# Attention stage of a fused four-part kernel: grid operations moved by one step, five copies moved to ScalarE, x turned inside k's product

## The chip, the cores and the metric

One core of a Trainium2 chip. The metric is the time of one execution on the device in microseconds, the median of repeated runs. All data is float32 but for a mask in bfloat16.

## What is computed

Eight examples of 512 x 512 pass through four parts. The change concerns the first two, and they run interleaved.

```
# 1, the grid: A, B are coefficient grids, f is one example
Af, Bf = A * f, B * f
df = -(grad(Af[0], 1) + grad(Af[1], 2)) + 0.5 * (
    grad2(Bf[0], 1) + grad2(Bf[1], 2) + 2 mixed second differences of Bf[2])
x = maximum(f + df * dt, 0)
# 2, attention, 16 heads of 32, and its feed-forward
x = ln(x) * (1 + scale) + shift
q, k, v = x @ Wq + bq, x @ Wk + bk, x @ Wv + bv
probs = softmax(where(mask, -inf, q @ k.T / sqrt(32) + attention_bias))
x = x + (probs @ v) @ Wo + bo
x = x + gelu2((ln(x) * g2 + beta2) @ W1 + b1) @ W2 + b2
# 3 a second feed-forward with a chosen expert's weights, 4 a gated low-rank response
```

## The kernel before

A first stage makes the grid of example 0. The attention stage then runs over 8 batches (examples), each in 16 steps: 4 chunks c of 4 heads by 4 row groups r of 128 query rows. A step is called by its number t = 4c + r in its batch. The two feed-forwards and the response follow in a third stage, which the change leaves alone.

The program order on every engine is the order in which the source writes the instructions (`pin`). One step i of the loop at line 1093 writes, in this order: a small GpSimd instruction that waits for the last grid operation on VectorE (`grid_gate`, line 731), then the additions of the mask to the next unit's bias on GpSimd (`add_mask`, line 970); every second step the products of probabilities and values (`values`, 1026); then twice, for u = 0 and 1 (two heads each): `turned` of the unit before (line 1008), `softmax` of this unit (line 990), and one piece of the side jobs; then the rest of the side jobs; after the last row group of a chunk `divide` (1048), which turns the reciprocals of the sums through PSUM and scales the context; `inverse` (1041); the bias load of three units ahead; the grid operations and their loads; and the four scores matmuls of the next unit (`scores`, 979). `softmax` reads the scores from PSUM on VectorE and takes the exponential on ScalarE; the scores of the next unit need the four score buffers back.

`turned` transposes one head's probabilities by four TensorE transposes into a PSUM tile of tag "tr", and copies it to SBUF: the first head of a pair on VectorE (line 1022), the second on ScalarE (line 1024). The tag "tr" has two buffers, which also serve `divide`, `x1_in` and `x1_back`.

The side jobs of a step (`fill`, line 908) are pieces of this batch's q (`q_block`, steps 0, 4, 8) and k (`k_block`, steps 1, 5, 9), the output products of the batch before (`o_block`, steps 2, 3, 6, 7), and in steps 10 to 15 the values, q and k of the next batch. In step 9 `x1_in` (line 601) turns the next example's x, chunk by chunk: four transposes into "tr", and a copy with scale and shift, for chunks 0 and 2 on VectorE (line 612), for 1 and 3 on ScalarE (line 610). It overwrites the four buffers of this batch's turned x, whose last readers are k's four matmuls of step 9. `x1_back` transposes x back in steps 11 to 14.

The grid of example n is made on VectorE while batches n - 2 and n - 1 run: `grid_step` (line 844) gives each step a place j, with j = 0 in step 8 of batch n - 2, j = 8 in step 0 of batch n - 1, and j = 16 in its step 8. The table GRID (line 821) says which operations are written at the end of a step with which j. A letter is an operation on a pair of rows (`grid_op`, line 759), most of them one VectorE instruction on 128 x 1024 elements with both inputs in SBUF; "hh" is eight small ones. In the steps that have `divide`, what stands before a "|" is written before it, and the rest after `inverse`. The operations written at the end of one step run at the beginning of the next. Coefficients for them are loaded by SP's queue at places of their own (`grid_loads`, line 719). For example 1 the first operations run in batch 0's step 0 (`grid_early`).

Of the kernel before, what the change touches and what calls it, by code (L numbers as in the profile page):

```python
# [20 lines left out]
NB = 8  # L21
S = 512
D = 512
P = 128
# [5 lines left out]
KC = D // P  # L30
# [514 lines left out]
def attention_stage(  # L545
# [13 lines left out]
    with ExitStack() as ctx:  # L559
# [6 lines left out]
        def mm(out, lhsT, rhs, start, stop):  # L566
            pin(nc.tensor.matmul(out, lhsT=lhsT, rhs=rhs, start=start, stop=stop))  # L567

        def tp(out, src):
            pin(nc.tensor.transpose(out, src, ident))  # L570
# [6 lines left out]
        def add_bv():  # L577
            pb = ps.tile([P, D], F32, name="pb", tag="m")
            for k in range(KC):
                mm(pb, bvr[:, k, :], w["Wo"][:, k, :], k == 0, k == KC - 1)  # L580
            pin(nc.vector.tensor_tensor(bo, pb, bo, ALU.add))


        mask, x1s, qs, ks, vs, cts = {}, {}, {}, {}, {}, {}
# [6 lines left out]
        def mask_out(b, r):  # L591
            m = pp.tile([P, S], BF16, name=f"mk_{b}_{r}", tag=f"mk{r}", bufs=1)
            pin(nc.scalar.activation(m, mask[b, r], AF.Copy, scale=NEG))
            mask[b, r] = m

        def load_mask(b, r):
            mask_in(b, r)
            mask_out(b, r)


        def x1_in(b, c):
            tag, bufs = ("tr", 2) if b or c < 2 else (f"s{c}", 1)
            tr = ps.tile([P, R, P], F32, name=f"xtr_{b}_{c}", tag=tag, bufs=bufs)
            for r in range(R):
                tp(tr[:, r, :], xt[b][:, r, c * P : (c + 1) * P])
            t = io.tile([P, S], F32, name=f"x1_{b}_{c}", tag="x1", bufs=4)
            tv, trv = t.rearrange("f (p r) -> f p r", r=R), tr.rearrange("f r p -> f p r")
            g, h = sc1[:, c, b : b + 1], shift[:, c, b : b + 1]
            if c % 2:
                pin(nc.scalar.activation(tv, trv, AF.Identity, bias=h, scale=g))  # L610
            else:
                pin(nc.vector.tensor_scalar(tv, trv, g, h, ALU.mult, ALU.add))
            x1s[b, c] = t

        def x1_back(b, r):
            tr = ps.tile([P, KC, P], F32, name=f"xb_{b}_{r}", tag="tr", bufs=2)
            for c in range(KC):
                tp(tr[:, c, :], x1s[b, c][:, r::R])
            pin(
                nc.vector.tensor_tensor(  # L620
                    xt[b][:, r, :], tr.rearrange("p c f -> p (c f)"), bo, ALU.add
                )
            )

        def block(out, lhsT, rhs):

            def half(h):
                for k in (2 * h, 2 * h + 1):
                    mm(out, lhsT(k), rhs(k), k == 0, k == KC - 1)
            return half  # L630

        def q_block(b, c, tag="m"):
            pr = ps.tile([P, S], F32, name=f"pq_{b}_{c}", tag=tag)
            half = block(
                pr, lambda k: w["Wq"][:, k, c * P : (c + 1) * P], lambda k: x1s[b, k]
            )
            yield half(0)
            yield half(1)
            t = pp.tile([P, S], F32, name=f"qt_{b}_{c}", tag="qt")
            pin(  # L640
                nc.vector.tensor_scalar(
                    t.rearrange("f (r p) -> f r p", r=R), pr.rearrange("f (p r) -> f r p", r=R),
                    bqk[:, 0, c : c + 1], QSCALE, ALU.add, ALU.mult,
                )
            )
            qs[b, c] = t

        def k_block(b, c, tag="m"):
            pr = ps.tile([P, S], F32, name=f"pk_{b}_{c}", tag=tag)
            half = block(  # L650
                pr, lambda k: w["Wk"][:, k, c * P : (c + 1) * P], lambda k: x1s[b, k]
            )
            yield half(0)
            yield half(1)
            t = pp.tile([P, S], F32, name=f"kt_{b}_{c}", tag="kt")
            pin(nc.scalar.activation(t, pr, AF.Identity, bias=bqk[:, 1, c : c + 1]))
            ks[b, c] = t

        def v_block(b, m, tag="m", bufs=1):
            pr = ps.tile([P, D], F32, name=f"pv_{b}_{m}", tag=tag, bufs=bufs)  # L660
            half = block(
                pr,
                lambda k: x1s[b, k][:, m * P : (m + 1) * P],
                lambda k: w["Wv"][:, k, :],
            )
            yield half(0)
            yield half(1)
            t = io.tile([P, D], F32, name=f"v_{b}_{m}", tag=f"v{m}", bufs=2)
            pin(nc.scalar.copy(t, pr))
            vs[b, m] = t  # L670
# [88 lines left out]
        def grid_op(n, op):  # L759
# [59 lines left out]


        GRID = {
            0: "q0 q1", 1: "e0 |", 2: "w0 c0 hh", 3: "C0", 4: "+0 -0", 5: "g0 |", 6: "G0 a0",
            7: "A0 b0 B0", 8: "x0 q2", 9: "e1 | w1 c1", 10: "C1 +1", 11: "-1 g1", 12: "G1 s0",
            13: "a1 | n0 A1 b1", 14: "B1 x1", 15: "s1", 16: "n1",
        }

# [77 lines left out]
        def grid_early(j):  # L904
            grid_sums(1, j)
            grid_loads(1, j)

        def fill(b, t):

            n = b + 1  # L910
            jobs = []
            if b == 0:
                if t == 0:
                    homes = (("m", 1), ("tr", 2), ("tr", 2), ("ctx", 1))
                    for m in range(4):
                        jobs.append(v_block(0, m, *homes[m]))
                        jobs.append(grid_early(j) for j in (m + 3,))
                    jobs.append(grid_early(7) for _ in range(1))
                    jobs.append(mask_out(0, r) for r in (2, 3))
                elif t == 2:  # L920
                    jobs.append(add_bv() for _ in range(1))
                elif t in (3, 4, 6, 7):
                    jobs.append(x1_back(0, (3, 4, 6, 7).index(t)) for _ in range(1))
            if t in (0, 4, 8):
                jobs.append(q_block(b, t // 4 + 1))
            elif t in (1, 5, 9):
                jobs.append(k_block(b, t // 4 + 1))
            elif t in (2, 3, 6, 7):
                if b:
                    jobs.append(o_block(b - 1, (2, 3, 6, 7).index(t)))  # L930
            elif n < NB:
                if t == 11:
                    jobs.append(q_block(n, 0))
                elif t == 13:
                    jobs.append(k_block(n, 0))
                else:
                    jobs.append(v_block(n, (10, 12, 14, 15).index(t)))
            if n < NB:
                if t == 9:
                    jobs.append(x1_in(n, c) for c in range(KC))  # L940
                if t in (11, 12, 13, 14):
                    jobs.append(x1_back(n, t - 11) for _ in range(1))
                if t >= 12:
                    jobs.append(load_mask(n, t - 12) for _ in range(1))
            elif t == 8:
                jobs.append(head_stats() for _ in range(1))
            elif t in (10, 11):
                jobs.append(head_norm(r) for r in (2 * t - 20, 2 * t - 19))
            elif t >= 12:
                jobs.append(head_turn(t - 12) for _ in range(1))  # L950
            for j in jobs:
                yield from j
# [55 lines left out]
        def turned(b, c, r, u):  # L1008

            bt = bias.pop((b, c, r, u))  # L1010
            for i in range(2):
                h = 2 * u + i
                if r % 2 == 0:
                    pts[b, c, r // 2, h] = pp.tile(
                        [P, KC, 2, P], F32, name=f"pt_{b}_{c}_{r}_{h}", tag=f"pt{h}", bufs=1
                    )
                pt = pts[b, c, r // 2, h]
                tr = ps.tile([P, KC, P], F32, name=f"tr_{b}_{c}_{r}_{h}", tag="tr", bufs=2)
                for k in range(KC):
                    tp(tr[:, k, :], bt[:, i, k * P : (k + 1) * P])  # L1020
                if i == 0:
                    pin(nc.vector.tensor_copy(pt[:, :, r % 2, :], tr))  # L1022
                else:
                    pin(nc.scalar.copy(pt[:, :, r % 2, :], tr))  # L1024
# [43 lines left out]
        n = len(units)  # L1068
# [14 lines left out]
        drain(q_block(0, 0))  # L1083
        grid_early(1)
        drain(k_block(0, 0, "ctx"))
        mask_out(0, 1)
        load_bias(*units[2])
# [5 lines left out]
        for i in range(n + 2):  # L1093
# [3 lines left out]
            jobs = fill(now[0], 4 * now[1] + now[2]) if now else iter(())  # L1097
# [783 lines left out]
```

## Time and profile before

| | us |
|---|---|
| median of 3 runs | 2771.0 |
| lowest and highest of them | 2770.07, 2774.91 |
| profiled execution | 2773.14 |
| its span, first to last instruction | 2771.4 |
| granted TensorE clock, share | 0.992 |
| first scores matmul of the attention stage | 71.0 |
| first scores matmul of its last step | 1103.6 |

The profile is of one execution. PE is the matmul, PEld the load of its weights, DVE VectorE, ACT ScalarE, POOL GpSimd; L1022 is line 1022 of the kernel. In the page's strip of 40 slices each digit is the busy share of one slice in tenths; a slice is 69.3 us long, so the attention stage fills the first 16. A group's line names what it writes and reads by the program's names: "tr" are turned probabilities in PSUM and "pt" their copy, "s" scores, "bt" bias and probabilities, "xtr" x being turned, "rb" the turned reciprocals. In timelines the bracket at the end is the idle time before an instruction and what ended it. The ends of matmuls are modelled, so consecutive ones can overlap by some tenths.

### The profile page before, as it was taken

The page shows a single profiled execution, that of the slowest core. Times are in us where ns is not written, and L with a number is a line of the kernel's source. Part 1 is how long each engine was busy: PE and PEld are TensorE (multiplying, and loading weights), DVE is VectorE, ACT ScalarE, POOL GpSimd, SP SyncE. Part 2 cuts the span into 40 slices and gives each one's busy share as a digit, 9 for nine tenths or more (in the row PEclk, how much of TensorE's full clock was granted, in tenths as well). Part 3 has the DMA queues.
Part 4 walks back from the last instruction along what each step waited for, and adds up shares of the span by engine and source line. Part 5 has one row for each costly group of instructions (what it writes and reads, how often), then busy time and mean ns, then how long its engine had stood idle before and what let it go on. Part 6 is the DMA issues. An engine that isn't in the chain of part 4 may idle for free.

```text
span 2771.4 us, 39819 instructions
## 1 busy us (share of the span) xinstructions
PE 2708.5 (98%) x14662; PEld 2009.6 (73%) x14662; DVE 1941.1 (70%) x3581; ACT 1004.9 (36%) x2137; POOL 1501.9 (54%) x1074
## 2 busy tenths in 40 slices
PE   7899999999999999999999999999999999999998
PEld 4455555555555554788888888888888888888886
DVE  7889898988888756577667666755456566566564
ACT  2566666666666666212111211211121221221221
POOL 3455555555555654466465555655636646646643
PEclk9999999999999999999999999999999999999998
DMA  8665757666666555542542543344133143142120
GB/s 317 234 208 169 240 179 238 192 219 214 193 231 193 162 155 171 173 114 65 160 126 40 154 134 85 101 145 133 58 126 114 58 156 114 58 156 99 59 76 31
DMA packets 190208, 405.27 MB, mean 146 GB/s; under 512 B 24024, under 2 KB 28704, under 8 KB 183742
## 3 DMA queue, kind: packets, MB, share of 16 engines
q1 hardware_dynamic: 186202, 391.97, 42.5%
q0 software_dynamic: 3360, 10.68, 3.1%
q8 instruction: 117, 1.92, 0.3%
q14 instruction: 77, 0.63, 0.1%
q10 hardware_dynamic: 452, 0.07, 0.0%
HBM read 366.97 MB, written 31.50 MB: 144 GB/s over the span
## 4 chain that ended last, share of the span: by engine, by line
PE 86%; DVE 10%; ACT 3%; DMA 1%; issue 1%; SPq 0%; ACTq 0%; POOL 0%; DVEq 0%
PE u L1164 28%; PE y L1164 28%; PE tr L570 7%; PE s L567 4%; PE ctx L567 4%; PE o L567 3%; PE pv L567 3%; PE pq L567 3%; PE pk L567 2%; DVE bt L997 2%; DVE x L687 2%; DVE pt L1022 1%; ACT bt L1002 1%; PE btr L1167 1%; PE ytr L1167 1%
## 5 line engine op out<-in xcount | busy, mean ns | idle before, releaser
L974 POOL TENSOR_TENSOR bt<-bt,mk 128x1024 f32<-128x1024 f32 x256 | 542.7, 2142 | 64.1 <-DMA bt<-in_bias 59.1
L1164 PE MATMUL y<-wo,act 128*128 128x256 f32 x2560 | 573.2, 380 | 0.0
L1164 PEld LDWEIGHTS y<-wo,act 128*128 128x128 f32 x2560 | 481.3, 190 | 70.0 <-issue 6.9
L1002 ACT ACTIVATE bt<-bt,mn 128x512 f32<-128x512 f32 x512 | 365.5, 715 | 112.1 <-DVE mn L997 112.1
L570 PEld LDWEIGHTS tr<-ident,bt 128*128 128x128 f32 x2048 | 228.1, 141 | 169.6 <-issue 116.8
L1164 PE MATMUL u<-bt,wi 128*128 128x256 f32 x1440 | 330.5, 379 | 0.0
L997 DVE CUSTOM_DVE_ANT_0 bt<-s,bt 128x512 f32<-128x512 f32 x512 | 330.5, 683 | 0.0
L1170 DVE TENSOR_TENSOR act<-u,u 128x512 f32<-128x512 f32 x256 | 173.3, 686 | 210.0 <-PE u L1164 132.3
L1164 PEld LDWEIGHTS u<-bt,wi 128*128 128x128 f32 x1440 | 273.5, 190 | 37.2
L570 PE MATMUL tr<-ident,bt 128*128 128x128 f32 x2048 | 280.4, 278 | 20.3 <-DVE pt L1022 8.5
L1022 DVE COPY pt<-tr 128x512 f32<-128x512 f32 x256 | 175.9, 687 | 113.0 <-PE tr L570 112.8
L1164 PE MATMUL u<-tb,ws 128*128 128x256 f32 x1024 | 242.2, 379 | 0.0
L1164 PE MATMUL y<-t,s 128*128 128x256 f32 x1024 | 234.2, 380 | 0.0
L1024 ACT COPY pt<-tr 128x512 f32<-128x512 f32 x256 | 148.3, 579 | 183.3 <-PE tr L570 181.2
L1164 PEld LDWEIGHTS u<-tb,ws 128*128 128x128 f32 x1024 | 194.3, 190 | 26.6 <-DVE tb L1170 0.2
L1173 POOL TENSOR_TENSOR t<-wo,t 128x512 f32<-128x512 f32 x64 | 104.5, 1648 | 200.1 <-PE y L1164 200.0
L1164 PEld LDWEIGHTS y<-t,s 128*128 128x128 f32 x1024 | 191.1, 190 | 24.1
L1484 ACT ACTIVATE act<-act,b 128x512 f32<-128x512 f32 x128 | 82.9, 711 | 292.8 <-DVE act L1170 292.8
L1484 ACT ACTIVATE act<-act,bi 128x512 f32<-128x512 f32 x128 | 83.8, 712 | 282.6 <-DVE act L1170 282.6
L567 PE MATMUL s<-kt,qt 32*128 32x512 f32 x1024 | 171.5, 644 | 2.2 <-DVE mn L997 1.4
L1170 DVE TENSOR_TENSOR x<-y,x 128x512 f32<-128x512 f32 x96 | 64.5, 685 | 154.2 <-PE y L1164 100.3
L1170 DVE TENSOR_TENSOR u<-u,u 128x512 f32<-128x512 f32 x192 | 131.2, 684 | 57.4 <-PE u L1164 57.3
(317 smaller groups left out, 4261.0 us busy)
## 6 DMA issues: line engine op xcount, KB each, us to landing
bt<-in_bias SPq DMA_DIRECT2D x256, 512.0 KB
wo<-in_W SPq DMA_DIRECT2D x32, 1024.0 KB
wi<-in_Wi SPq DMA_DIRECT2D x32, 1024.0 KB
wo<-in_Wo_e SPq DMA_DIRECT2D x32, 1024.0 KB
wi<-in_W SPq DMA_DIRECT2D x28, 1024.0 KB
gq<-coef_q SPq DMA_DIRECT2D x21, 512.0 KB
x1d<-x SPq DMA_DIRECT2D x8, 1024.0 KB
x<-x1d SPq DMA_DIRECT2D x8, 1024.0 KB
```

What stands on the lines that cost most here:

```text
L567: pin(nc.tensor.matmul(out, lhsT=lhsT, rhs=rhs, start=start, stop=stop))
L570: pin(nc.tensor.transpose(out, src, ident))
L687: pin(nc.vector.tensor_tensor(out, x, y, op))
L974: nc.gpsimd.tensor_tensor(bt, bt, mask[b, r][:, None, :].to_broadcast([P, 2, S]), ALU.add)
L997: nc.vector.tensor_tensor_reduce(bt[:, i, :], ss[h], bt[:, i, :], -1.0, 3.0e38, ALU.add, ALU.min, mn)
L1002: nc.scalar.activation(bt[:, i, :], bt[:, i, :], AF.Exp, bias=mn, scale=-1.0, accum_out=sums[b, c, r][:, h : h + 1],)
L1022: pin(nc.vector.tensor_copy(pt[:, :, r % 2, :], tr))
L1024: pin(nc.scalar.copy(pt[:, :, r % 2, :], tr))
L1164: pin(nc.tensor.matmul(out, lhsT=lhsT, rhs=rhs, start=start, stop=stop))
L1170: pin(nc.vector.tensor_tensor(out, x, y, op))
L1173: pin(nc.gpsimd.tensor_tensor(out, x, y, op))
L1484: nc.scalar.activation(acts[g][:, k, :], acts[g][:, k, :], func, bias=bi[:, j : j + 1])
```

## The change

It touches four places, all in the attention stage.

- GRID: in the places j = 1 to 7 operations are moved to an earlier step; their order among each other stays.
- `turned`: for the first head pair, the first head's copy is made by ScalarE instead of VectorE where 4c + r is 1, 3, 5, 7 or 15.
- `k_block` gets an argument turn, used in step 9 for the next example: after k's third matmul it calls `x1_in` for chunks 0 and 1, after the fourth and the copy of k for chunks 2 and 3. Its second pause comes after the third matmul then, instead of the fourth.
- `fill` gives this argument and no longer adds the four calls of `x1_in` after k's block.

```diff
-        def k_block(b, c, tag="m"):
+        def k_block(b, c, tag="m", turn=None):
+
             pr = ps.tile([P, S], F32, name=f"pk_{b}_{c}", tag=tag)
-            half = block(
-                pr, lambda k: w["Wk"][:, k, c * P : (c + 1) * P], lambda k: x1s[b, k]
-            )
-            yield half(0)
-            yield half(1)
+            for k in range(KC):
+                mm(
+                    pr, w["Wk"][:, k, c * P : (c + 1) * P], x1s[b, k], k == 0, k == KC - 1
+                )
+                if k == 1 or k == (2 if turn else 3):
+                    yield
+                if turn and k == 2:
+                    turn(0)
+                    turn(1)
             t = pp.tile([P, S], F32, name=f"kt_{b}_{c}", tag="kt")
             pin(nc.scalar.activation(t, pr, AF.Identity, bias=bqk[:, 1, c : c + 1]))
             ks[b, c] = t
+            if turn:
+                turn(2)
+                turn(3)
...
         GRID = {
-            0: "q0 q1", 1: "e0 |", 2: "w0 c0 hh", 3: "C0", 4: "+0 -0", 5: "g0 |", 6: "G0 a0",
-            7: "A0 b0 B0", 8: "x0 q2", 9: "e1 | w1 c1", 10: "C1 +1", 11: "-1 g1", 12: "G1 s0",
+            0: "q0 q1", 1: "e0 | w0", 2: "c0 hh C0", 3: "+0", 4: "-0 g0", 5: "G0 |", 6: "a0 A0",
+            7: "b0 B0", 8: "x0 q2", 9: "e1 | w1 c1", 10: "C1 +1", 11: "-1 g1", 12: "G1 s0",
             13: "a1 | n0 A1 b1", 14: "B1 x1", 15: "s1", 16: "n1",
         }
...
-                jobs.append(k_block(b, t // 4 + 1))
+                turn = (lambda c: x1_in(n, c)) if t == 9 and n < NB else None
+                jobs.append(k_block(b, t // 4 + 1, turn=turn))
...
-                if t == 9:
-                    jobs.append(x1_in(n, c) for c in range(KC))
...
-                if i == 0:
+                if i == 0 and not (u == 0 and 4 * c + r in (1, 3, 5, 7, 15)):
                     pin(nc.vector.tensor_copy(pt[:, :, r % 2, :], tr))
```

## The prediction, made before the change was run

> **What bounds the kernel now.** I read the page first, then the stretches table step by step, then the chain of waits inside the steps that stood out, then the engines' timelines around each wait.
>
> ```profile
> PE 2708.5 (98%) x14662; PEld 2009.6 (73%) x14662; DVE 1941.1 (70%) x3581; ACT 1004.9 (36%) x2137; POOL 1501.9 (54%) x1074
> ...
> DVE  7889898988888756577667666755456566566564
> ```
>
> TensorE is busy for 98% of the span, so only what makes it wait is to be had. VectorE is near its limit in the first 14 slices only, the attention stage, which holds the whole change. There the scores matmuls cut the trace into 128 steps; from batch 1 to 6 the 16 step times repeat within 0.3 us (6.91, 8.92, 7.43, 8.98, 6.59, 8.92, 7.49, 8.98, 6.41, 11.99, 6.41, 8.74, 6.88, 9.18, 6.88, 8.27 in batch 3: 129 us). Batch 7 has no grid work beside it and is the measure of an unhindered step. The stretches table, whose columns are the window, its length and each engine's busy time, has steps 2 and 3 of batch 7, then steps 2, 3 and 9 of batch 3, then step 9 of batch 7:
>
> ```profile
> 1007.04:1013.45 6.41, 6.41 (x33) 3.41 (x32) 4.48 (x12) 4.90 (x13) 3.92 (x3) 1.00 0.52 150
> 1013.45:1021.72 8.27, 8.27 (x65) 4.35 (x64) 4.59 (x12) 4.51 (x13) 4.10 (x3) 1.00 0.44 126
> 491.57:499.00 7.43, 6.62 (x33) 3.39 (x32) 6.55 (x14) 3.92 (x11) 2.82 (x3) 1.00 0.66 202
> 499.00:507.99 8.99, 8.99 (x66) 4.74 (x65) 7.68 (x18) 5.30 (x14) 5.92 (x4) 1.00 0.53 175
> 546.38:558.37 11.99, 11.27 (x85) 6.69 (x85) 9.33 (x20) 8.97 (x20) 4.38 (x3) 1.00 1.00 362
> 1057.91:1066.62 8.71, 8.71 (x69) 4.84 (x69) 7.76 (x21) 4.73 (x14) 4.37 (x3) 1.00 0.96 357
> ```
>
> Against batch 7, steps 0 to 9 lose 0.50, 0.21, 1.02, 0.71, 0.18, 0.21, 1.08, 0.71, 0.00 and 3.28 us; steps 10 to 15 lose nothing but the transposes of x1_back. A busy PE hides waits: step 3's scores take 1.85 us instead of 1.14 although PE reads busy. The chain of waits in step 2 shows who is late:
>
> ```profile
> 493.02 0.69 DVE ct L1056
> 493.71 0.09 DVE rs L1043
> 493.80 1.11 DVE gq L687
> 494.91 1.13 DVE gc L687
> 496.04 0.61 DVE pt L1022
> 496.65 0.04 issue
> 496.70 0.66 PE tr L570 x4
> ```
>
> Two grid operations and then the copy of the turned probabilities keep VectorE until 496.64; the next transpose needs that PSUM buffer. Step 9's TensorE:
>
> ```profile
> 554.72 1.04 PE L570 MATMUL xtr<-ident,x 128*128 128x128 f32 x8
> 556.22 1.34 PE L570 MATMUL xtr<-ident,x 128*128 128x128 f32 x8 [0.47 <-DVE x L612]
> 557.78 0.66 PE L570 MATMUL rb<-ident,rw 128*128 128x128 f32 x4 [0.22 <-DVE x L612]
> ```
>
> The four turns of x go through two PSUM buffers, and each waits for the one two before it to be copied out. Step 0's VectorE:
>
> ```profile
> 604.58 1.19 DVE L687 TENSOR_TENSOR x<-x,ga 128x1022 f32<-128x1022 f32 x1
> 605.69 1.22 DVE L687 TENSOR_TENSOR gb<-gb,gf 128x1024 f32<-128x1024 f32 x1
> 606.95 1.22 DVE L687 TENSOR_TENSOR x<-x,gb 128x1022 f32<-128x1022 f32 x1
> 608.09 0.68 DVE L1022 COPY pt<-tr 128x512 f32<-128x512 f32 x1
> ```
>
> Three grid operations (A0 b0 B0) stand ahead of the copy that frees the buffer; TensorE waits for it until 608.91.
>
> [...] 0.69 us (VectorE copy) and 0.58 us (ScalarE copy). [...] the grid sum of 1.19 us that starts at 500.29 ends at 501.64, 1.09 us after GpSimd's mask addition ends at 500.55. [...]
>
> **The change part by part.** Each term is TensorE time in one batch.
>
> *Five copies to ScalarE.* old is the unit before, so 4c+r of 1, 3, 5, 7, 15 are handled in steps 2, 4, 6, 8 and in step 0 of the next batch. VectorE loses one copy there, 0.60 us from start to start; ScalarE gains 0.58 us. ScalarE idles where it is put (2.67 us before 497.28 in step 2), and has the first two copies done by about 495.2, before the second transposes at 495.29. Behind the moved copy, which waits for the transposes, ScalarE has the other copy and the exponentials, and these wait for VectorE until 497.28 anyway. What is late next in step 2 is VectorE's score chain: two score operations, a copy, two score operations run on from 495.96 instead of 496.56, and the last scores matmul waits for the last of them, 499.08 instead of 499.68. So steps 2 and 3 together gain 0.60, not the 1.73 that they lose. Step 6 is alike on VectorE. On ScalarE two normalizations (525.95 to 527.46) stand ahead of both copies: they end near 528.48, and the second half of the transposes starts 0.13 us earlier than 528.68; the score chain again ends 0.60 earlier. In steps 3 and 7 the mask addition doesn't move with it, so the first grid operation still ends 1.09 us after it; the slack before the next copy (0.45 us idle in step 3) takes most: I take 0.55 for steps 6 and 7. Steps 4 and 5 lose only 0.39 and 0.60 covers it: 0.39. Step 8 ends with the scores 0.16 late: 0.16.
>
> *Grid one ahead.* The order of the operations is the same; w0, C0, +0, g0, G0 and A0 come one step sooner, -0, a0, b0 and B0 stay. Step 0 has two instead of three, so VectorE is 1.2 + 0.6 us ahead and loses no more: 0.71 (steps 0 and 1). The other end is step 9, whose late part gets w0. It sits behind the reciprocal, from 559.79; the copy of step 10 would start 0.77 us later, the score chain has an idle 0.69 us (its wait for the transposes at 562.73) and ends 0.05 later, at the scores' need: 0. GpSimd's gate in step 10 waits for w0, so the mask additions start 2.2 us later and overlap c0 of step 11: about 0.5 us on VectorE, where C0 replaces w0. The copy there would end near 4.65 us into the step and is needed at 5.58: hidden. Without that cover it would be up to 1.2 us a batch. Loads stay in place: in batch 2 g's is issued at 422.2 and used at 460.9, so one step sooner still leaves 30 us, and c0's buffer is released sooner, so SP's queue of bias loads is held less, not more.
>
> *x turned around k's last matmul.* No instruction more or less: 16 transposes of 0.109 us, 4 copies, 2 matmuls of 0.43 us are only interleaved. After the second transposes k's third pair runs 553.00 to 553.86, two turns until 554.73 (their buffers are free at 553.46 and 553.84), the fourth pair until 555.60. VectorE is free of scores at 554.67 and copies turn 0 by 555.48; ScalarE, after its exponentials, copies turn 1 from 555.52 to 556.29. Turn 2 starts at 555.60, turn 3 at 556.34; turn 2's copy follows after 0.70 us, 556.30 to 557.11; the reciprocals' transposes start at 557.16 instead of 557.78: gain 0.62. Floor 0 if ScalarE's copy of k, behind turn 1, mattered; ceiling 12.0 - 8.7 - 1.7 = 1.5 us. I take 0.62.
>
> Sum: 0.60 + 0.55 + 0.39 + 0.16 + 0.71 + 0.62 = 3.03 us a batch, six batches 18.2. Batches 1 and 5 lose 0.25 more in step 8, which goes too: 0.5. Batch 0 waits for x1_back and the bias product as well; its steps 4 and 6 show the chain through the moved copy (0.60 each), and step 9 is the same 0.62: 1.8. Batch 7 has no waits to lose: 0. Total 20.5 us. The profiled execution took 2773.1 us (span 2771.4), 2.1 above the median; 2773.1 - 20.5 = 2752.6, beside the median 2771.0 - 20.5 = 2750.5.
>
> **The rivals.**
> 1. More: the score waits in steps 2, 3, 6 and 7 go altogether. Another 6 x (1.13 + 1.24) = 14 us: 2736. Against it: VectorE's chain from ct on is unbroken.
> 2. Less: ScalarE takes the place of VectorE as the one that frees the transposes' buffers, so steps 2, 3, 6 and 7 gain nothing, and half of step 9 is lost: 6 x 1.15 + 7 x 0.31 = 9 us back: 2760. For it: both copies then stand in one in-order queue, and which buffer a transpose gets is not in the source.
> 3. Slower: the mask additions, held up by gates that now come later, fall on the grid operations of the next step[...]. The trace has the worst of it at 80.27, a sum of 3.03 instead of 1.20 us. With a slack of 1.1 us before TensorE waits, 0.73 us would get through; in the seven steps from 10 to 0, in six batches, 31 us: 2781. It decides from 0.5 us a step. Against it: steps 11 to 15 keep their number of operations.
> 4. Nothing: the waits come back elsewhere in the same step: 2771.
>
> **How the numbers follow.** Forecast 0.60 (own range 2745 to 2756), more 0.08, less 0.19, slower 0.09, nothing 0.04. Beyond 0.2%, 5.5 us, a measurement tells a difference: faster 0.87, same 0.04, slower 0.09. The range takes in the first three, 2735 to 2764, and leaves out 0.13.
>
> **What would show it.** Step times of batch 3: steps 0 and 1 at 6.41 and 8.71, 4 and 5 the same, 2 with 3 near 15.8, 6 with 7 near 15.9, step 9 near 11.2, steps 10 to 15 unchanged. Steps 10 or 11 longer would show the grid's new place as a cost; a PE wait for ScalarE's copy in steps 2 or 6 would show rival 2; a VectorE grid operation over 2 us in steps 10 to 15, rival 3.

## The result, and the profile after

| | before | after |
|---|---|---|
| median of the runs measured side by side, us | 2772.95 (2770.07 to 2775.46) | 2753.39 (2751.49 to 2756.82) |
| profiled execution, us | 2773.1 | 2754.3 |
| its span, us | 2771.4 | 2752.5 |

The ratio of the times is 0.9931 with a 95% interval of 0.9914 to 0.9948: the change saves 19.6 us. Predicted were 20.5 us and 2750.5. Of the 2.9 us between the two medians, 2.0 lie in the median of the kernel before, which came out higher than in the runs shown first, and 0.9 in the saving.

The page of the kernel after, busy times of the engines:

```profile
PE 2699.4 (98%) x14662; PEld 2006.5 (73%) x14662; DVE 1931.6 (70%) x3541; ACT 1024.0 (37%) x2177; POOL 1502.1 (55%) x1074
```

Forty instructions left VectorE (3581 to 3541) and forty came to ScalarE (2137 to 2177): five copies in each of eight batches. For a saving of 19 us that is all this page says. TensorE's busy time fell by 9 us only, less than half of the saving, so the page's shares do not show where the rest came from. The steps do. Cut at the scores matmuls as in the prediction, in us, batch 3:

| steps | before | after | saved | predicted |
|---|---|---|---|---|
| 0 and 1 | 15.83 | 15.12 | 0.71 | 0.71 |
| 2 and 3 | 16.41 | 15.82 | 0.59 | 0.60 |
| 4 and 5 | 15.51 | 15.11 | 0.40 | 0.39 |
| 6 and 7 | 16.48 | 16.33 | 0.15 | 0.55 |
| 8 and 9 | 18.40 | 17.61 | 0.79 | 0.16 + 0.62 |
| 10 to 15 | 46.35 | 46.35 | 0.00 | 0 |
| whole batch | 128.97 | 126.33 | 2.64 | 3.03 |

Batches 1 to 6 together went from 774.4 to 758.2 us, 16.2 less. The rest of the saving in this execution is scattered: 2.2 in batch 0, 1.3 in batch 7, 0.3 ahead of the first scores, and 1.1 lost in the third stage. The section on the cause and the last one say why those do not count as effects of the change.

The stretches table of the kernel after, for steps 2, 3, 6, 7 and 9 of batch 3 (window, its length, busy time and instructions of PE, PEld, VectorE, ScalarE and GpSimd, granted clock, DMA share, GB/s):

```profile
483.08:489.49 6.41, 6.41 (x34) 3.41 (x33) 5.53 (x11) 3.98 (x10) 1.79 (x2) 1.00 0.70 234
489.49:498.90 9.41, 9.41 (x66) 4.91 (x65) 8.62 (x18) 5.72 (x16) 6.92 (x5) 1.00 0.53 168
514.01:521.65 7.64, 6.81 (x33) 3.30 (x32) 6.69 (x14) 6.54 (x16) 2.62 (x3) 1.00 0.42 125
521.65:530.34 8.69, 8.69 (x65) 4.61 (x64) 8.02 (x17) 5.49 (x13) 4.85 (x4) 1.00 0.54 183
536.75:547.95 11.20, 10.95 (x85) 6.56 (x84) 9.17 (x20) 8.81 (x20) 4.38 (x3) 1.00 1.01 369
```

Step 2 fell from 7.43 to the 6.41 of the unhindered batch, but step 3 grew from 8.99 to 9.41: 0.4 of the 1.0 us moved on by a step, and there the PE column reads 9.41 of 9.41, fully busy, although an unhindered step takes 8.27. Step 6 did not fall at all (7.50 to 7.64). Looking at step 2 alone would overstate the gain, and the PE column would hide what is left.

The chain of waits in step 2, which before ran through two grid operations and a copy on VectorE, holds nothing but TensorE now:

```profile
484.22 1.02 PE tr L570 x8
485.25 1.72 PE o L567 x4
486.96 0.87 PE tr L570 x8
```

TensorE's timeline in step 9, which answers to the three lines of before:

```profile
544.12 1.04 PE L570 MATMUL xtr<-ident,x 128*128 128x128 f32 x8
545.00 1.02 PE L567 MATMUL pk<-x,Wk 128*128 128x512 f32 x2
545.86 1.40 PE L570 MATMUL xtr<-ident,x 128*128 128x128 f32 x8
547.37 0.66 PE L570 MATMUL rb<-ident,rw 128*128 128x128 f32 x4
```

The fourth pair of k stands between the two halves of the turns and covers the copies of the first half; the brackets with waits of 0.47 and 0.22 us are gone. In step 0 VectorE has two grid operations left of the three, b0 from 594.16 and then B0:

```profile
595.46 1.23 DVE L695 TENSOR_TENSOR x<-x,gb 128x1022 f32<-128x1022 f32 x1
596.60 0.69 DVE L1004 CUSTOM_DVE_ANT_0 bt<-s,bt 128x512 f32<-128x512 f32 x1
```

Behind them comes a score operation and no copy at all: this is also a unit whose copy (15) went to ScalarE. Which of the two cured the step is a question for an experiment.

### The profile page after: what moved, and what is told of

It reads as the page before. It is cut to its first block, busy times and chain, and to the rows that moved or that the text cites. A ratio compares the mean times of both kernels' runs of the same rounds, so it can differ in the third digit from the quotient of the medians.

```text
span 2752.5 us, 39875 instructions
## 1 busy us (share of the span) xinstructions
PE 2699.4 (98%) x14662; PEld 2006.5 (73%) x14662; DVE 1931.6 (70%) x3541; ACT 1024.0 (37%) x2177; POOL 1502.1 (55%) x1074
## 4 chain that ended last, share of the span: by engine, by line
PE 91%; DVE 5%; ACT 2%; DMA 1%; issue 1%; SPq 0%; ACTq 0%; POOL 0%; DVEq 0%
PE u L1171 28%; PE y L1171 28%; PE tr L570 8%; PE s L567 5%; PE ctx L567 4%; PE pq L567 4%; PE pv L567 3%; PE o L567 3%; PE pk L567 3%; PE btr L1174 1%; PE l L251 1%; ACT bt L1009 1%; DVE x L695 1%; DVE bt L1004 1%; PE ytr L1174 1%
## 5 line engine op out<-in xcount | busy, mean ns | idle before, releaser
L1031 ACT COPY pt<-tr 128x512 f32<-128x512 f32 x296 | 167.8, 581 | 166.8 <-PE tr L570 163.8
L1029 DVE COPY pt<-tr 128x512 f32<-128x512 f32 x216 | 148.5, 687 | 98.7 <-PE tr L570 87.4
```

## The experiments

The step times of batches 1 to 6 repeat within 0.05 us in each profiled execution, with few exceptions, so each experiment is read from them; times given with one decimal are sums over these six batches unless a span is named. Single runs of one kernel differ by up to 5.4 us, more than most of these effects.

### The three parts, each alone

Each of the first three kernels is the kernel before with one part of the change.

e1, the five copies:

```diff
-                if i == 0:
+                if i == 0 and not (u == 0 and 4 * c + r in (1, 3, 5, 7, 15)):
```

> The kernel before with the five copies on ScalarE alone. If the three parts of the change act on separate waits: steps 2+3 15.82 us, 4+5 15.12, 6+7 16.33, 8 6.41 as with the whole change, step 9 11.8, and steps 0+1 15.2 (of the 0.71 us that they lose, the copy's 0.60 is enough for nearly all), steps 10 to 15 as before; 1.9 us a batch, span near 2759. If the copies only help together with the moved grid: steps 0+1 stay at 15.83 and the span is over 2763.

e2, the grid:

```diff
-            0: "q0 q1", 1: "e0 |", 2: "w0 c0 hh", 3: "C0", 4: "+0 -0", 5: "g0 |", 6: "G0 a0",
-            7: "A0 b0 B0", 8: "x0 q2", 9: "e1 | w1 c1", 10: "C1 +1", 11: "-1 g1", 12: "G1 s0",
+            0: "q0 q1", 1: "e0 | w0", 2: "c0 hh C0", 3: "+0", 4: "-0 g0", 5: "G0 |", 6: "a0 A0",
+            7: "b0 B0", 8: "x0 q2", 9: "e1 | w1 c1", 10: "C1 +1", 11: "-1 g1", 12: "G1 s0",
```

> The kernel before with the moved grid operations alone. If the parts act on separate waits: steps 0+1 15.12 (0.71 us less), all other steps as before (step 9 12.0, step 10 6.41, step 11 8.74); span near 2767. If the operation put at the end of step 9 costs in this order of work: steps 10 or 11 longer by up to 1.2 us, span 2771 or more.

e3, x turned inside k's product, with `k_block` as in the change:

```diff
-                jobs.append(k_block(b, t // 4 + 1))
+                turn = (lambda c: x1_in(n, c)) if t == 9 and n < NB else None
+                jobs.append(k_block(b, t // 4 + 1, turn=turn))
...
-                if t == 9:
-                    jobs.append(x1_in(n, c) for c in range(KC))
```

> The kernel before with x turned around k's last matmul alone. If the parts act on separate waits: step 9 from 12.0 to 11.37 us in batches 0 to 6, everything else as before, span near 2767. If step 9's gain came from VectorE being ahead through the other parts: step 9 stays over 11.8 and the span near 2771.

Measured, batch 3, us:

| steps | before | e1 copies | e2 grid | e3 turn | after |
|---|---|---|---|---|---|
| 0 and 1 | 15.83 | 15.23 | 15.11 | 15.83 | 15.12 |
| 2 and 3 | 16.41 | 15.81 | 16.41 | 16.41 | 15.82 |
| 4 and 5 | 15.51 | 15.11 | 15.51 | 15.51 | 15.11 |
| 6 and 7 | 16.48 | 16.34 | 16.48 | 16.48 | 16.33 |
| 9 | 11.99 | 11.89 | 11.98 | 11.30 | 11.20 |
| batches 1 to 6, saved | | 11.1 | 4.8 | 4.2 | 16.2 |
| span | 2771.4 | 2757.4 | 2763.0 | 2767.3 | 2752.5 |

The parts act in separate steps and add up, with one exception. Their sum is 11.1 + 4.8 + 4.2 = 20.1 us. Steps 0 and 1 are cured twice: e1 saves 0.60 there and e2 0.72, together they save 0.71. Taking 6 x 0.60 = 3.6 off leaves 16.5, beside the 16.2 measured for all. So beside the grid's move the copy of unit 15 has nothing left to gain in that step, and the grid's move gains nothing anywhere else. Step 9's 0.79 is 0.69 from the turns and 0.10 from the copies. And the shortfall in steps 6 and 7 belongs to the copies alone: e1 shows 16.34 without the other two parts.

### Why steps 6 and 7 gain so little

The chain of waits in step 6, first of the kernel before (start, length, what), where step 6 begins at 523.49, then of the kernel after, where it begins at 514.01:

```profile
520.36 0.02 DVE mn L997
520.38 0.02 issue
520.40 1.06 ACT bt L1002 x3
...
522.39 1.47 ACT bt L1002 x4
...
524.94 0.69 DVE ct L1056
```

```profile
511.26 0.02 DVE mn L1004
511.28 0.02 issue
511.31 0.67 ACT bt L1009
...
513.30 1.42 ACT bt L1009 x4
...
515.80 0.69 DVE ct L1063
```

It is the same chain, with the rest of ScalarE's exponentials and its copies of probabilities, of k and of the turned reciprocals in the lines left out, but measured from the step's begin it is late. The context's scaling on VectorE (ct) starts 1.45 us into the step before and 1.79 after. Backwards: the exponentials (bt) ahead of it end 0.37 us into the step before, 0.71 after; and VectorE's score operation (mn) from which ScalarE runs on to ct's input without idle time ends 3.11 us ahead of the step before (520.38), 2.73 ahead of it after (511.28). The reason is in step 5. TensorE's wait there is gone (8.92 to 8.71 us), so step 6 begins 0.21 sooner; VectorE's own work in step 5, a grid sum and the statistics s0, did not get shorter. From the reciprocal to the first copy it takes 3.91 us instead of 3.73, since the sum itself went from 1.28 to 1.46 beside a mask addition on GpSimd. The sum, before and after:

```profile
515.43 1.28 DVE L687 TENSOR_TENSOR x<-x,gg 128x1024 f32<-128x1024 f32 x1
```

```profile
506.17 1.46 DVE L695 TENSOR_TENSOR x<-x,gg 128x1024 f32<-128x1024 f32 x1
```

The theory: the copy moved in step 6 is worth what it was thought to be, and the late hand-over from step 5 eats 0.34 of it. If so, the kernel after without that one copy must have steps 6 and 7 slower than the kernel before had.

```diff
-                if i == 0 and not (u == 0 and 4 * c + r in (1, 3, 5, 7, 15)):
+                if i == 0 and not (u == 0 and 4 * c + r in (1, 3, 7, 15)):
```

> The changed kernel with the copy of unit 5 (the one in step 6) back on VectorE; the other four stay. If VectorE's score chain sets step 6's end, and starts late because step 5 hands VectorE and ScalarE over later: steps 6+7 16.9 us (0.60 over the changed kernel, and over the 16.47 of the kernel before), span 3.6 us over the changed kernel's 2752.5. If instead the two copies one behind the other on ScalarE are what is late in step 6: steps 6+7 at 16.33 or below, span the same or lower.

The stretches of steps 6 and 7 in e4:

```profile
514.58:522.43 7.85, 7.02 (x34) 3.29 (x33) 6.90 (x15) 5.67 (x14) 2.82 (x3) 1.00 0.42 121
522.43:531.40 8.97, 8.97 (x65) 4.73 (x64) 7.90 (x19) 6.12 (x15) 5.14 (x4) 1.00 0.57 193
```

Together 16.82 us: 0.34 worse than before's 16.48, as large as the delay read from the chain, and 0.49 worse than after. In e4, ct starts 1.79 us into step 6, as late as in the kernel after. So the copy is worth 0.49, the late hand-over costs 0.34, and 0.49 - 0.34 is the 0.15 that the change saved.

The 0.11 by which the copy falls short of 0.60 is lost behind the scores. Counted from the begin of step 6, VectorE's last score operation that the scores of step 7 wait for ends at 8.53 us in e4 and at 7.92 in the kernel after: 0.61 sooner. Then step 7 loses some of it. In e4, VectorE's first grid sum there and TensorE's second transposes are these:

```profile
523.70 1.36 DVE L695 TENSOR_TENSOR x<-x,gb 128x1022 f32<-128x1022 f32 x1
528.72 1.04 PE L570 MATMUL tr<-ident,bt 128*128 128x128 f32 x8
```

In the kernel after, with ScalarE's part between them:

```profile
522.53 1.96 DVE L695 TENSOR_TENSOR x<-x,gb 128x1022 f32<-128x1022 f32 x1
526.04 1.06 ACT L802 ACTIVATE x<-x 128x1024 f32<-128x1024 f32 x1 [2.91 <-DVE x L796]
527.39 0.59 ACT L1031 COPY pt<-tr 128x512 f32<-128x512 f32 x1 [0.29 <-ACT x L802]
527.55 1.15 PE L570 MATMUL tr<-ident,bt 128*128 128x128 f32 x8
```

More of a mask addition lies beside the sum: GpSimd's addition ends at 523.41, and the sum 1.08 us later, 1.96 us long instead of 1.36. Behind it the grid's activation on ScalarE starts 4.39 us into step 7 instead of 4.19, and with it the copy that frees a buffer of the transposes. These take 1.15 us instead of 1.04, which is the 0.11. This part is read from the two traces; no run changed the sum alone.

### Taking work out of step 5

If step 5's VectorE hands over late, moving the statistics out of it should bring step 6 down. In e5 a1 takes the place of the statistics s0, which move to the beginning of step 6, and n0 (which needs them) and GpSimd's power of the variance move with them.

```diff
-            7: "b0 B0", 8: "x0 q2", 9: "e1 | w1 c1", 10: "C1 +1", 11: "-1 g1", 12: "G1 s0",
-            13: "a1 | n0 A1 b1", 14: "B1 x1", 15: "s1", 16: "n1",
+            7: "b0 B0", 8: "x0 q2", 9: "e1 | w1 c1", 10: "C1 +1", 11: "-1 g1", 12: "G1 a1",
+            13: "s0 | A1 b1", 14: "n0 B1 x1", 15: "s1", 16: "n1",
...
-            if j in (12, 15):
+            if j in (13, 15):
```

> The changed kernel with a1 in the place of the statistics s0 in step 5, s0 ahead of divide instead of a1, and the normalization n0 one step later (in step 7). If steps 6+7 kept most of their loss because step 5's VectorE chain, led by G1 and s0, hands over 0.34 us late: step 5's chain has 0.45 us less, steps 6+7 16.0 us instead of 16.33, span near 2750.5. If the two normalizations on ScalarE ahead of the copies in step 6 don't matter and neither does the start: 16.3, span 2752.5.

A miss with a lesson. Step 6 came down to 6.41 us, the unhindered value, and then step 7 took 10.41: together 16.82, 0.49 worse than after. VectorE's timeline in step 7 of e5 (the bracket is the idle time ahead and what ended it), and GpSimd's:

```profile
521.93 0.17 DVE L1050 RECIPROCAL rs<-sums 128x4 f32<-128x4 f32 x1
523.58 0.16 DVE L818 SCALAR_TENSOR_TENSOR gsh<-gmv,grs 128x2 f32<-128x2 f32 x1 [1.47 <-POOL grs L850]
```

```profile
518.66 4.22 POOL L981 TENSOR_TENSOR bt<-bt,mk 128x1024 f32<-128x1024 f32 x2
522.84 0.70 POOL L850 TENSOR_TENSOR grs<-grs,mhalf 128x2 f32<-128x2 f32 x1
```

n0 begins with a tiny VectorE instruction (gsh) that needs GpSimd's power of the variance, and that power stands behind 4.22 us of mask additions in GpSimd's queue. VectorE stood still for 1.47 us with everything behind the tiny instruction waiting. In step 6 the hand-over is on time again, ct starts 1.45 us into it as in the kernel before; in step 7 the gain is lost to a wait that the edit made itself. But e5 moved two things out of step 6: the late hand-over, and n0's two normalizations on ScalarE, which stand there for 1.52 us ahead of the copies that the transposes wait for. It can't tell which of them brought step 6 to 6.41. e9 takes the wait of step 7 away: the same edit, with n0 one step later still.

```diff
-            13: "s0 | A1 b1", 14: "n0 B1 x1", 15: "s1", 16: "n1",
+            13: "s0 | A1 b1", 14: "B1 x1", 15: "n0 s1", 16: "n1",
```

> The changed kernel with a1 in step 5, s0 ahead of divide, and n0 only in step 8, two steps after s0, so that no engine waits for GpSimd's power in step 7. If the lost 2.1 us of step 7 in the run with n0 in step 7 was that wait, and the late hand-over of step 5 is what the change left in step 6: steps 6+7 15.9 us (16.33 less the 0.41 by which that run's scores ended sooner), step 8 6.41, span near 2750. If the hand-over isn't the cause: 6+7 at 16.3.

Steps 6 and 7 took 15.90 us, the value asked for: against after a saving of 0.43 a batch, 2.8 us over batches 1 to 6. The wait was the whole of e5's miss, 16.82 - 15.90 = 0.92 us a batch; it was 0.9 of the 2.1 us that step 7 of e5 lost, and step 7 still takes 9.50.

Like e5, e9 has no normalizations in step 6. That the 0.43 comes from the hand-over and not from them is read from VectorE, whose score operations the scores of step 7 wait for. In the kernel after it has no idle time from ct (515.80) to the last of these (521.93), so the copies that came late on ScalarE did not hold it. In e9 ct starts 1.44 us into step 6 instead of 1.79:

```profile
514.46 0.69 DVE L1063 TENSOR_TENSOR ct<-ctx,rbs 128x512 f32<-128x512 f32 x1 [0.20 <-ACT rbs L1060]
```

The last score operation ends 7.51 us into the step instead of 7.92, and 0.35 of these 0.41 are ct's. A run with the normalizations moved and nothing else was not made.

### What is left in steps 2 and 3

The prediction left steps 2 and 3 with 1.13 us against the unhindered batch, bound by VectorE's unbroken chain. e6 takes one grid operation out of that chain: c1 goes from step 2's beginning to step 1's.

```diff
-            7: "b0 B0", 8: "x0 q2", 9: "e1 | w1 c1", 10: "C1 +1", 11: "-1 g1", 12: "G1 s0",
+            7: "b0 B0", 8: "x0 q2 c1", 9: "e1 | w1", 10: "C1 +1", 11: "-1 g1", 12: "G1 s0",
```

> The changed kernel with c1 one step sooner, in step 1 instead of step 2. If VectorE's chain of two grid operations in step 2 is what still holds the scores of step 3 by 1.13 us: steps 2+3 14.7 us instead of 15.82, step 1 unchanged at 8.71 (its next transposes wait for nothing up to 1.1 us), span near 2746. If the added operation comes before c1's data or is late for step 1's transposes: steps 0+1 over 15.4, and the span above 2748.

Steps 2 and 3 fell from 15.82 to 14.84 (6.53 and 8.31), all others stayed: 5.8 us over the six batches, more than either the grid's or the turns' part of the change saved. One VectorE operation of about 1.1 us is worth 0.98 us there, which shows that the chain was unbroken; and in its new place it costs nothing. e7, with e5's and e6's edits together, says whether they are independent:

> The two edits before together. If they act on separate waits: steps 2+3 14.7, 6+7 16.0, others as in the changed kernel, span near 2744.

They are independent: 14.85 in steps 2 and 3, and 16.83 in steps 6 and 7. The 16.0 and the span were missed (2749.4 us instead of 2744), since e5's wait is in it. e8 moved the whole second half of the grid ahead by one operation, with n0 and GpSimd's power where e5 has them:

```diff
-            7: "b0 B0", 8: "x0 q2", 9: "e1 | w1 c1", 10: "C1 +1", 11: "-1 g1", 12: "G1 s0",
-            13: "a1 | n0 A1 b1", 14: "B1 x1", 15: "s1", 16: "n1",
+            7: "b0 B0", 8: "x0 q2 c1", 9: "e1 | w1", 10: "C1 +1 -1", 11: "g1 G1",
+            12: "a1 A1", 13: "s0 | b1", 14: "n0 B1 x1", 15: "s1", 16: "n1",
```

> The changed kernel with all second-half grid operations one ahead: c1 in step 1, -1 in step 3, G1 in 4, a1 and A1 in 5, s0 ahead of divide, b1 alone in 6, n0 in 7. If VectorE's chain behind the scaled context is the bound of steps 2 and 6: steps 2+3 near 14.7 and 6+7 near 14.9 us, 4+5 still 15.12, span near 2737. If GpSimd's later mask additions and the three operations of step 3 take over: steps 2+3 or 4+5 longer by 0.5 to 1 us and the span over 2742.

Its span was 2746.8 us, where 2737 was expected. Steps 6 and 7 took 15.69, with n0's wait still in them. Steps 2 and 3 took 15.08 and steps 4 and 5 15.32, worse than e6 by 0.24 and 0.21: with three operations in place 10 the beginning of step 3 is the crowded one, and the copy behind them starts 5.0 us into the step. Another 2.1 of the 9.8 us by which the span was missed are one step, step 9 of batch 1 with 13.29 us instead of 11.20, whose cause was not tested. The load has to be spread over the steps; moving everything ahead moves the crowd.

### A version that is faster than both

e10 keeps what held: c1 in place 8, two operations in each of the places 10 and 11 at most, A1 out of step 6's beginning, and n0 late, with GpSimd's power in place 13 as in e5.

```diff
-            7: "b0 B0", 8: "x0 q2", 9: "e1 | w1 c1", 10: "C1 +1", 11: "-1 g1", 12: "G1 s0",
-            13: "a1 | n0 A1 b1", 14: "B1 x1", 15: "s1", 16: "n1",
+            7: "b0 B0", 8: "x0 q2 c1", 9: "e1 | w1", 10: "C1 +1", 11: "-1 g1",
+            12: "G1 a1 A1", 13: "s0 | b1", 14: "B1 x1", 15: "n0 s1", 16: "n1",
```

> The changed kernel with c1 in step 1, G1 a1 A1 in step 5, s0 ahead of divide with b1 alone behind it in step 6, n0 in step 8. If VectorE's chain is the bound and what is put into steps 1 and 5 is covered: steps 2+3 14.85, 4+5 15.12, 6+7 15.1 to 15.2, 8 6.41, 2.15 us a batch, span near 2740, ratio to the kernel before near 0.9885. If step 5's three operations are late for its transposes: 4+5 longer by 0.3 or more, span over 2743.

Median 2738.62 us (2737.57 to 2739.39), ratio to the kernel before 0.9877 with an interval of 0.986 to 0.9893. The change as made has 0.9931, so this saves about three quarters more. The stretches of steps 6 and 7 in e10:

```profile
506.56:513.22 6.66, 6.63 (x34) 3.39 (x33) 6.29 (x17) 5.37 (x13) 3.42 (x4) 1.00 0.52 145
513.22:521.65 8.43, 8.43 (x66) 4.37 (x65) 7.66 (x16) 5.22 (x13) 6.24 (x5) 1.00 0.53 185
```

They are within 0.3 us of the unhindered 6.41 and 8.27, and steps 2 and 3 (6.52 and 8.32) within 0.12. Against the changed kernel no instruction went: VectorE does the same work (3541 instructions in both), at times at which TensorE hardly waits for it. What is left above the unhindered batch is mostly step 9's 2.5 us and the transposes of x1_back.

## Why the prediction held, and where it was off

**Steps 0 and 1, 0.71: right in size, incomplete in cause.** The prediction credited the grid with all of it. e2 shows that the grid suffices (0.72), and e1 that the copy of unit 15 alone gives 0.60 too. Had the two been added, the sum would have been 3.6 us too large; the prediction avoided that by counting the step's loss once.

**Steps 2 and 3, 0.60: right.** "What is late next in step 2 is VectorE's score chain" is what the step times show: the whole 1.0 us leaves step 2, 0.4 comes back in step 3, and e6's shorter chain takes most of the rest.

**Steps 4 and 5, and the copies' last term: right.** 0.40 against 0.39. The 0.16 put down to step 8 came out as 0.10 in step 9, since step 8 was at 6.41 already. The 0.25 that batches 1 and 5 lose in step 8 (6.66) went in batch 5 only; in batch 1 it came back in step 7, which took 8.96 us instead of 8.69.

**Steps 6 and 7, 0.55: the mis-sized term, 0.15 measured.** The step was "the score chain again ends 0.60 earlier", with "I take 0.55 for steps 6 and 7". It treated step 6 as a copy of step 2. But the prediction itself had step 5 end 0.21 sooner, and did not ask whether what step 6 needs from VectorE in step 5 would come sooner too. It does not; the end of a wait on TensorE moved the need forward and the supply stayed. e4 separates the two: the copy is worth 0.49, the late supply costs 0.34. Over six batches the term is 2.4 us short of its 3.3, nearly all of the 2.5 between 18.7 predicted for batches 1 to 6 (18.2 + 0.5) and the 16.2 measured.

**Step 9, 0.62: right.** 0.69 in e3, and the order of turns, pair and copies is the one that was worked out. ScalarE's copy of k did not matter. The ceiling of 1.5 us is 1.6 from the rounded figures beside it; nothing rests on it.

**What was costed at nothing.** w0's new place at the end of step 9, the later mask additions and C0 in step 11 cost nothing: steps 10 to 15 take 46.35 us in both kernels. Beside the later additions c0 did take longer, by 0.72 us (1.94 instead of 1.22) where the author's estimate was about 0.5, and it stayed hidden as said.

**Batches 0 and 7.** Predicted 1.8 and 0; the profiled executions differ by 2.2 and 1.3. Batch 7's steps are equal in both kernels but for 11 (11.58 and 10.08) and 12 (6.71 and 6.97), whose code the change leaves alone, so its 1.3 measures the scatter, and batch 0's sum of 2.2 is no confirmation. Its single steps do confirm the term: 4 and 6, which the prediction names with 0.60 each, went from 10.01 to 9.41 and from 8.13 to 7.53 us, in e1 as well, and step 9 from 11.83 to 11.29 (0.54). Steps 1 and 8 beside them moved by 1.4 us up and 1.6 down; in each, the slower execution has 3.41 us at half the granted clock.

**The total.** By the steps the change is worth 16.2 us in batches 1 to 6 and 1.7 in batch 0, 17.9 in all. That the medians differ by 19.6, only 0.9 from the 20.5 predicted, is in part luck: the runs of one kernel lie up to 5.4 us apart.

**The rivals.** More: the waits in steps 3, 6 and 7 are still there, and only the further edits of e10 remove most of them. Less: in step 2 TensorE waits for no copy and in step 9 the turns gained in full; in step 6 the transposes do wait for ScalarE's copy, which was to be the sign of this rival, but they waited for it before as well, as these lines of before and after show:

```profile
528.08 1.26 PE L570 MATMUL tr<-ident,bt 128*128 128x128 f32 x8 [0.70 <-ACT pt L1024]
```

```profile
518.94 1.06 PE L570 MATMUL tr<-ident,bt 128*128 128x128 f32 x8 [0.75 <-ACT pt L1031]
```

In both kernels the copy stands behind n0's two normalizations on ScalarE, which after the change start 0.34 us later in the step. Slower: longer grid sums do occur, 1.96 us in step 7 and 1.46 in step 5 where they took 1.35 and 1.28 before; they cost some tenths in steps 5 to 7. In steps 10 to 15, where the rival put them, the longest is c0 with 1.94 us, and it cost nothing. After the change each of the three ends 1.08 us after the mask addition that GpSimd runs beside it (end of the addition and of the grid operation: 506.55 and 507.63 in step 5, 523.41 and 524.49 in step 7, 555.08 and 556.16 in step 11). Why was not tested. Nothing: the waits did not come back in the same steps but for the 0.4 in step 3 and what step 6 kept.

Whether more "tr" buffers would help was not shown: no run changed their number. In e10 steps 2, 3, 6 and 7 come within 0.3 us of the unhindered times with the same two.

## What to carry to other kernels

When a wait is taken away on the engine that sets the end, everything that the next step needs from other engines is needed sooner by as much (here 0.21 us, at the begin of step 6): ask for each following step whether the supply moves too, or the gain of the next edit is partly spent before it starts. Two edits that free the same step count once: here 0.60 and 0.72 us alone, 0.71 together. Before a tiny instruction is moved ahead in an engine's program order, look at what stands ahead of its own producer: here 0.70 us of work on GpSimd, behind 4.2 us of other work, stopped VectorE for 1.47 us.

## What was not expected of the hardware

TensorE's granted clock falls to half for 3.41 or 6.83 us at a time in the attention stage, in one execution and not in another of the same instructions. Step 11 of batch 7 has the same code in all the kernels. The stretches table of that step, first of the kernel before, then of e2 (the clock is the third number from the end):

```profile
1070.56:1082.14 11.58, 10.34 (x58) 4.80 (x57) 5.12 (x15) 5.86 (x16) 9.45 (x5) 0.71 0.39 144
```

```profile
1065.67:1074.11 8.44, 6.87 (x58) 3.66 (x56) 4.87 (x14) 5.76 (x14) 8.43 (x5) 1.00 0.44 137
```

The 58 TensorE instructions took 10.34 us of busy time in one and 6.87 in the other. The 32 products of probabilities and values among them took 3.64 us and 1.93. The clock's records are at 0.5 for 6.83 us in the step before, for 3.41 us after (10.08 us) and not at all in e2 (8.44). Batch 0 has such stretches too, 10.2 us in all, before and after alike. From batch 1 to batch 6 the granted clock is 1.00 in before, after, e2 and e3. TensorE's waits alone do not explain the stretches: ahead of the one in step 11 it waits for 0.78 and then for 1.13 or 1.14 us in before, after and e2 alike. In batches 1 to 6 of the kernel before, where TensorE's single waits reach 0.8 us, the clock stays full. What decides whether a stretch comes was not tested. With 3.1 us between e2 and before in one step of equal code, they are nearly as large as the turns' whole part of this change: a difference of a few us between two single executions can be this alone, which is why the steps of batches 1 to 6, and medians, carry the verdicts here.
